# Layer 3 of a four-layer image network: gates ahead of another batch's taps, taps in PSUM, folding shared with GpSimd, a new order of two interleaved images

## The chip, the cores and the metric

The kernel runs on one core of one Trainium2 chip. The metric is the device time of one launch in microseconds (us), as the median of several runs. The core has a matrix engine (TensorE, PE in the profile, with its weight loads as PEld), a vector engine (VectorE, DVE), an activation engine (ScalarE, ACT), a general engine (GpSimd, POOL), a synchronisation engine (SyncE, SP) on whose queue this kernel issues its transfers, and 16 DMA engines. Each engine works through its own queue in order; semaphores make one wait for another. SBUF is the on-chip memory, PSUM the accumulation memory that TensorE writes.

## What is computed

Eight images of 192 channels and 64 x 64 pixels, in 32-bit floats, pass four layers. Layers 0 and 2 are two-dimensional state-space scans in four directions, with norms, 1 x 1 convolutions and gates around them. Layer 1 works pixel by pixel. Layer 3 is the one that the change touches:

```python
xc = _conv1x1(x, w1, b1)                       # 192 -> 64 channels
for nw in (4, 8, 12):
    s = H // nw; k = s + H % nw                # (s, k): (16, 16), (8, 8), (5, 9)
    hi = (jnp.arange(nw) * s)[:, None] + jnp.arange(k)[None, :]
    patches = xc[:, :, hi][..., hi]
    u3 = patches.transpose(0, 1, 3, 5, 2, 4).reshape(N, C * k * k, nw * nw)
    u4 = u3.reshape(-1, C, k, k)               # the same bytes, read as samples
    a = _se(_conv1x1(u4, w2, b2), wse1, wse2) + _dwconv3x3(u4, wpos, bpos)
    a3 = a.reshape(N, C * k * k, nw * nw)
    p = a3.reshape(N, C, k, k, nw, nw).transpose(0, 1, 4, 2, 5, 3)
    folded = jnp.zeros((N, C, H, W)).at[:, :, hidx, widx].add(p)
    out_list.append(folded / cnt)
out = _conv1x1(jnp.concatenate(out_list, axis=1) + x, w3, b3)
```

`_se` multiplies each sample by a sigmoid gate per channel, made from the sample's means by two small matrices; `_dwconv3x3` is a depthwise 3 x 3 convolution, nine taps per pixel.

## The kernel before

For each image there are a scan of layer 0, the end of layer 0 and layer 1, a scan of layer 2, and then `between(b, b + 1)`. The scans are ordered by hand and take most of the time. `between` is different: it interleaves two generators, `behind` for image b (the end of layer 2, all of layer 3, the output) and `ahead` for image b + 1 (the load, norm, dense 1 x 1 convolutions and depthwise convolution that open layer 0). The generators are stepped in turn, one step of each; the order in which they are stepped is the order in which the program is written, and a scheduler derives from it and from the buffers the fixed order of instructions on each queue. So there is one `ahead` without a partner at the start, seven mixed stages, and one `behind` without a partner at the end. A pool of PSUM is shared: a "wide" tile holds two rows of 512 floats, a "narrow" one holds one. In a mixed stage each generator has one wide and two narrow buffers, alone three and two.

`behind` first loads the four scan results (`ys`, L745, 6 MB), joins and norms them in four steps, and makes `xc` in four steps. It copies the windows with VectorE or ScalarE into `p2` and `p01` and stores them to `u3` in device memory (L793). The same bytes are read back as samples: this is what turns windows into samples. `samples(i, p, passes, t_u, t_p)` (L818) then does, for one pass, the following:

- loads the samples into `u4`, a view of the room named by `t_u` (L832), clears a padded tile in the room named by `t_p` on GpSimd (L836) and copies the samples into it with ScalarE (L838);
- for each group of samples multiplies by `w2` (L846), adds a bias in place (L850), and sums over pixels (L854); two small matmuls and a Sigmoid (L862) give the gate;
- for each group runs the nine taps: four on TensorE into a narrow PSUM tile (L870); GpSimd writes `acc` = u4 x gate (L876) and adds two terms that ScalarE makes (L884, L885); VectorE adds three taps to `acc` in SBUF (L887), and last combines PSUM, bias and `acc` into `u4` (L890);
- stores `u4` to `a3` in device memory (L897).

Window 2 goes in two passes of six groups, windows 0 and 1 in one pass of four each, twenty groups an image. A group is 128 partitions of 486 or 512 floats. There are five rooms, t0 to t3 and u, which the passes take in turn, so a load into a room waits for the store out of it. After the second pass window 2 is read back from `a3` (L795) and, after the third, added to a cleared image (memset L905) at its window positions by VectorE (L914, 18 instructions, nine rows of the window in two parts each), then scaled where windows overlap (L921, L924). After the fourth pass windows 0 and 1 are read back together into t0 and added to x (L932): window 0 by VectorE and GpSimd in alternation, window 1 by VectorE. Four steps of final matmuls (L939, L462, L465) and the output follow. `ahead` has its own dense convolution with stores to `a_scr`, its depthwise convolution (L1012 on TensorE, L1019 on VectorE in place in PSUM), stores to `vs` (L1026, L1058, L1060) and the transposed columns (`put_columns`, L1068 to L1078).

Of the kernel before, what the change touches and what calls it, by code (L numbers as in the profile page):

```python
# [7 lines left out]
F32 = mybir.dt.float32  # L8
AF = mybir.ActivationFunctionType
ALU = mybir.AluOpType  # L10
# [4 lines left out]
P = 128  # L15
CA, CB = 128, 64
S = 64
T = S * S
W = 1024
NCH = T // W  # L20
Q = 512
# [19 lines left out]
def tile_net(ctx: ExitStack, tc: tile.TileContext, a: dict, out: bass.AP):  # L41
    nc = tc.nc
# [23 lines left out]
    a3 = [dram.tile([64, k * k * nw * nw], F32, name=f"a3_{nw}") for nw, _, k in WINDOWS]  # L66
# [357 lines left out]
    def half(h):  # L424
        return slice(h * CB, (h + 1) * CB)
# [300 lines left out]
    PE_TAPS = 4  # L726


    def behind(b, pool, wk, psp, table):

        wide_, narrow_ = psp
        x = new_pair(pool, "x")

        def room(tag, n):
            return pool.tile([P, n], F32, name=tag, tag=tag)
# [45 lines left out]
        def view(flat, i, n=None):  # L781
            nw, s, k = WINDOWS[i]
            return flat.rearrange("p (a b i j) -> p a b i j", a=n or k, b=k, i=nw)

        def move_windows(i, t, dram, store):
            if i < 2:
                pairs = [(t[half(i)], dram[i])]
            else:
                pairs = [(t[half(0)], dram[2][:, 0 : 45 * 144])]
                pairs += [(t[half(1)][:, 0 : 36 * 144], dram[2][:, 45 * 144 :])]  # L790
            for s, d in pairs:
                if store:
                    nc.sync.dma_start(out=d, in_=s)  # L793
                else:
                    nc.sync.dma_start(out=s, in_=d)  # L795
# [19 lines left out]
            move_windows(i, p01, u3, True)  # L815


        def samples(i, p, passes, t_u, t_p):  # L818

            nw, s, k = WINDOWS[i]  # L820
            kk, nsmp = k * k, nw * nw
# [37 lines left out]
            ps = wide_("se2")[:, 0]  # L859
            nc.tensor.matmul(ps[:, :mh], se2, hid, start=True, stop=True)  # L860
            gate = wk.tile([P, mh], F32, tag="gate3", name="gate3")
            nc.scalar.activation(gate, ps[:, :mh], AF.Sigmoid)  # L862
            yield "pass"
            for g in range(0, mh, per):
                ms = slice(g, g + per)
                ps = narrow_("pw")
                tap = [divmod(t, 3) for t in range(9)]
                tap = [pad[:, g // per, dy : dy + k, dx : dx + k, :] for dy, dx in tap]
                for t in range(PE_TAPS):
                    nc.tensor.matmul(  # L870
                        ps[:, : per * kk], taps[:, t, :], tap[t],
                        start=(t == 0), stop=(t == PE_TAPS - 1),
                    )
                acc = wk.tile([P, Q], F32, tag="acc", name="acc")[:, : per * kk]
                turned = u4[:, ms, :].rearrange("p m j -> p j m")
                nc.gpsimd.tensor_tensor(  # L876
                    acc.rearrange("p (j m) -> p j m", m=per), turned,
                    gate[:, ms].unsqueeze(1).to_broadcast([P, kk, per]), ALU.mult,
                )
                rows = acc.rearrange("p (r x) -> p r x", r=k)  # L880
                tap = [t.rearrange("p r q m -> p r (q m)") for t in tap]
                for t in range(PE_TAPS, PE_TAPS + 2):
                    term = wk.tile([P, Q], F32, tag="term", name="term")[:, : per * kk]
                    nc.scalar.mul(term.rearrange("p (r x) -> p r x", r=k), tap[t], pos[:, t : t + 1])  # L884
                    nc.gpsimd.tensor_tensor(acc, acc, term, ALU.add)  # L885
                for t in range(PE_TAPS + 2, 9):
                    nc.vector.scalar_tensor_tensor(  # L887
                        rows, tap[t], pos[:, t : t + 1], rows, ALU.mult, ALU.add
                    )
                nc.vector.scalar_tensor_tensor(  # L890
                    turned, ps[:, : per * kk].rearrange("p (j m) -> p j m", m=per), bpos,
                    acc.rearrange("p (j m) -> p j m", m=per), ALU.add, ALU.add,
                )
                yield "conv"
            for h in range(2):
                m0 = h * (nsmp // 2) + p * mh
                nc.sync.dma_start(out=af[:, m0 : m0 + mh, :], in_=u4[half(h)])  # L897

        yield from samples(2, 0, 2, "u", "t2")
        yield from samples(2, 1, 2, "t0", "t1")  # L900
        p2 = room("t1", size["t1"])
        move_windows(2, p2, a3, False)
        yield from samples(0, 0, 1, "u", "t2")
        acc = room("t2", size["t2"])[:, 0:T]
        nc.gpsimd.memset(acc, 0.0)  # L905
        yield from samples(1, 0, 1, "t0", "t3")


        nw, s, k = WINDOWS[2]
        for ki in range(k):  # L910
            h = ki // 5
            for kj0, kj1 in ((0, s), (s, k)):
                to = image_rows(acc[half(h)], s, nw, ki, kj0, kj1)
                nc.vector.tensor_tensor(  # L914
                    to, to, view(p2[half(h)], 2, 5)[:, ki - 5 * h, kj0:kj1], ALU.add
                )
            yield "fold"

        both = acc[:, s * S : s * nw * S].rearrange("p (g r w) -> p g r w", r=s, w=S)
        both = both[:, :, 0 : k - s, :]  # L920
# [1 line left out]
        both = acc.rearrange("p (h w) -> p h w", w=S)[:, :, s : s * nw]  # L922
        both = both.rearrange("p h (g r) -> p h g r", r=s)[:, :, :, 0 : k - s]
        nc.vector.tensor_scalar_mul(both, both, 0.5)  # L924
        p01 = room("t0", size["t0"])
        for i in range(2):
            nw, s, k = WINDOWS[i]
            move_windows(i, p01, a3, False)
            for ki in range(k):
                to = image_rows(x[0][half(i)], s, nw, ki, 0, k)  # L930
                eng = nc.gpsimd if i == 0 and ki % 2 else nc.vector
                eng.tensor_tensor(to, to, view(p01[half(i)], i)[:, ki], ALU.add)  # L932
            yield "fold"
        two = w3[0][:, 320:384]
        for u in range(NU):
# [144 lines left out]
    def between(done, todo):  # L1080

        with (
            tc.tile_pool(name="bt_w", bufs=2) as wk,
            tc.tile_pool(name="bt_ps", bufs=1, space=PSUM) as psp,
            ExitStack() as stack,
        ):
            gens = []
            table = tc.keep_in_program_order(nc.scalar.preload_act_table_set(EXP_LN))
            alone = done is None or todo is None
            for name, fn, b in (("c", behind, done), ("a", ahead, todo)):  # L1090
                if b is None:
                    continue
                pool = stack.enter_context(tc.tile_pool(name="bt_" + name, bufs=1))

                def wide_(what, name=name):
                    return psp.tile(
                        [P, 2, Q], F32, tag="pa" + name, name=what + name, bufs=3 if alone else 1
                    )

                def narrow_(what, name=name):  # L1100
                    return psp.tile([P, Q], F32, tag="pb" + name, name=what + name, bufs=2)

                gens.append(fn(b, pool, wk, (wide_, narrow_), table))
            while gens:
                for g in list(gens):
                    if next(g, None) is None:
                        gens.remove(g)

    layer1_weights()
    between(None, 0)  # L1110
    for b in range(nimg):
# [131 lines left out]
```

## Time and profile before

| what | us |
|---|---|
| median of 3 runs (27051.87 to 27094.4) | 27072.46 |
| the profiled execution's own time | 27067.12 |
| its span | 27065.3 |
| first mixed stage, from the first load of ys to the next scan's first load | 471.4 (3071.97 to 3543.39) |
| the last image alone, from the first load of ys to the end | 367 (26698.29 to 27065.3) |

The times are in us from the start of the span. A group line of the profile names the line of the code, the engine, the operation, the tile written and the tiles read, the shape, how often it ran, its busy time and the mean of one in ns, and then the idle time of its engine just before it with what ended that. A line of the timeline has the start, the length, the engine and the group; the brackets hold the idle time before and what released it. A line of the table of waits has the engine and line that waited, the one waited for, the sum in us, how many times and the longest.

The engines' totals over the whole span:

```profile
PE 23913.7 (88%) x108424; PEld 10495.5 (39%) x108424; DVE 21238.1 (78%) x24245; ACT 14494.4 (54%) x23064; POOL 19174.4 (71%) x7516
```

They are averages over scans and stages between them: the scans fill TensorE, VectorE and GpSimd, the stages between them are emptier.

### The profile page before, as it was taken

Reading aid. Unit: us, or ns where it says so; the run is one execution under the profiler, and the core shown is the slowest. Engines: PE = TensorE matmul, PEld = TensorE weight load, DVE = VectorE, ACT = ScalarE, POOL = GpSimd, SP = SyncE. Lnnn points to the kernel's source line nnn. Section 1 sums busy time; section 2 is a strip of 40 time slices with the busy share of each in tenths; the row PEclk is TensorE's granted clock in tenths of the full one; section 3 lists DMA queues with packets and bytes.
Section 4 is the critical chain, followed back from the end, with each engine's and each line's share of the span. In section 5 each row is a group of like instructions: output and inputs, shape, how many; then the busy total and the mean of one; then the engine's idle time right before and its main releaser. Section 6 shows DMA issues by size and latency. Waiting matters only on the chain.

```text
span 27065.3 us, 306873 instructions
## 1 busy us (share of the span) xinstructions
PE 23913.7 (88%) x108424; PEld 10495.5 (39%) x108424; DVE 21238.1 (78%) x24245; ACT 14494.4 (54%) x23064; POOL 19174.4 (71%) x7516
## 2 busy tenths in 40 slices
PE   9979889798897988979889798897988979889797
PEld 3424334243342433424334243342433424344243
DVE  7959779597795978959789597895978959788596
ACT  5646556465564655646456464564645546455464
POOL 6929679295792957929579295792957939579395
PEclk8989989899898998989989899898998989989898
DMA  5636556265563655626556365563655636556364
GB/s 158 200 92 197 146 160 201 91 194 147 161 198 90 197 146 164 201 90 199 142 164 198 92 197 142 162 198 93 197 142 165 194 98 197 139 165 195 96 197 130
DMA packets 1239264, 4286.14 MB, mean 158 GB/s; under 512 B 427920, under 2 KB 454384, under 8 KB 839408
## 3 DMA queue, kind: packets, MB, share of 16 engines
q1 hardware_dynamic: 1237744, 4266.51, 53.5%
q8 instruction: 877, 14.37, 0.2%
q14 instruction: 643, 5.27, 0.1%
HBM read 3810.80 MB, written 450.72 MB: 157 GB/s over the span
## 4 chain that ended last, share of the span: by engine, by line
PE 29%; DVE 24%; issue 5%; POOL 5%; ACT 3%; DMA 2%; SPq 0%; DVEq 0%; POOLq 0%; ACTq 0%
DVE da L296 16%; PE py L326 10%; PE u L278 8%; POOL da L308 2%; PE pa L462 2%; DVE dg L193 1%; DVE u L293 1%; DVE tmp L291 1%; POOL acc L885 1%; PE pa L465 1%; PE misc L208 1%; ACT da L241 1%; POOL acc L876 1%; PE misc L226 1%; PE pac L462 1%
## 5 line engine op out<-in xcount | busy, mean ns | idle before, releaser
L308 POOL TENSOR_TENSOR da<-da,ct 128x2048 f32<-128x2048 f32 x3072 | 13920.5, 4531 | 856.9 <-DVE tmp L291 475.5
L296 DVE TENSOR_TENSOR_SCAN da<-da,u 128x1024 f32<-128x1024 f32 x6144 | 14046.0, 2287 | 447.4 <-ACT da L251 162.1
L326 PE MATMUL py<-da,ident 128*128 128x512 f32 x18432 | 9658.6, 642 | 59.9 <-POOL da L308 59.9
L278 PE MATMUL u<-dg,dtt 32*128 32x256 f32 x65536 | 7247.2, 410 | 663.5 <-DVE da L296 656.3
L241 ACT ACTIVATE da<-dt,neg_a 128x512 f32<-128x512 f32 x12288 | 7612.3, 708 | 16.3
L278 PEld LDWEIGHTS u<-dg,dtt 32*128 32x128 f32 x65536 | 4137.1, 164 | 5382.7 <-issue 3538.8
L326 PEld LDWEIGHTS py<-da,ident 128*128 128x128 f32 x18432 | 3258.5, 197 | 4117.5 <-issue 3958.1
L218 POOL TENSOR_TENSOR dtx<-dt,vt 128x512 f32<-128x512 f32 x768 | 979.0, 1276 | 4187.7 <-ACT dt L214 4017.4
L311 POOL TENSOR_TENSOR da<-da 128x512 f32<-128x512 f32 (+1 forms) x3072 | 3484.4, 1134 | 240.9
L228 ACT COPY dtt<-misc 128x512 f32<-128x512 f32 x768 | 450.1, 586 | 3001.5 <-PE misc L226 3001.5
L293 DVE TENSOR_TENSOR u<-u,tmp 128x16 f32<-128x16 f32 x6048 | 1106.2, 183 | 951.9 <-PE u L278 354.8
L231 ACT COPY dtt<-misc 32x512 f32<-32x512 f32 x3072 | 1772.1, 577 | 46.2
L193 DVE TENSOR_TENSOR dg<-msk,misc 128x1024 f32<-128x1024 f32 x1024 | 1223.3, 1197 | 251.5 <-PE misc L183 222.1
L155 ACT ACTIVATE xd<-misc,msk 128x512 f32<-128x512 f32 x256 | 176.0, 687 | 1806.9 <-PE misc L151 1806.9
L291 DVE TENSOR_TENSOR tmp<-da,da 128x16 f32<-128x16 f32 x5376 | 945.0, 176 | 144.7
L214 ACT ACTIVATE dt<-misc 128x512 f32<-128x512 f32 x768 | 430.7, 595 | 1055.7 <-PE misc L210 1010.7
L836 POOL MEMSET t<- 128x4356 f32 (+2 forms) x32 | 99.8, 3120 | 1186.2 <-DVE t L810 1029.7
L870 PE MATMUL pwc<-t,l3taps 128*128 128x486 f32 (+1 forms) x1280 | 723.1, 703 | 242.6 <-DVE u L890 144.5
L887 DVE SCALAR_TENSOR_TENSOR acc<-t,l3p,acc 128x486 f32<-128x486 f32 (+1 forms) x480 | 479.7, 1026 | 415.8 <-POOL acc L885 412.1
L141 PE MATMUL misc<-vt,wxt 128*128 128x512 f32 x512 | 318.0, 706 | 361.9 <-DMA vt<-vs 361.9
L208 PE MATMUL misc<-xd,wdt 64*128 64x512 f32 x1024 | 600.4, 699 | 13.4 <-ACT xd L155 13.4
L462 PE MATMUL pa<-sqa,mean_w 128*128 128x512 f32 x384 | 304.7, 939 | 344.5 <-ACT sqa L502 344.5
(285 smaller groups left out, 18922.6 us busy)
## 6 DMA issues: line engine op xcount, KB each, us to landing
ct<-cd SPq DMA_DIRECT2D x2048, 1024.0 KB
ct<-cd SPq DMA_DIRECT2D x2048, 512.0 KB
vt<-vs SPq DMA_DIRECT2D x768, 256.0 KB
yp<-yo SPq DMA_DIRECT2D x384, 256.0 KB
yo<-yp SPq DMA_DIRECT2D x384, 256.0 KB
ys<-yo SPq DMA_DIRECT2D x384, 256.0 KB
yt<-ys SPq DMA_DIRECT2D x96, 512.0 KB
t<-ys SPq DMA_DIRECT2D x96, 512.0 KB
```

The lines of the kernel that those rows point to most:

```text
L193: nc.vector.tensor_tensor(dg[m, o][:, at], msk[:, 0:32].unsqueeze(1).unsqueeze(1).to_broadcast(shape), bts[m, o][:, at, r * 8 : r * 8 + 8] ...
L218: nc.gpsimd.tensor_tensor(dtx[k], dts[k], vt[k // 3][:, units[k][3], :], ALU.mult)
L231: nc.scalar.copy(dtt[k][q * 32 : q * 32 + 32, 1], src if q < 3 else src[:, ::-1])
L241: nc.scalar.activation(das[k][:, :, n, :], dts[k].rearrange("p (s t) -> p s t", t=SB), AF.Exp, scale=neg_a[:, v, d, n : n + 1],)
L278: nc.tensor.matmul(u[ch, r * 8 : r * 8 + 8, e:SB:2], dtt[k][rows, r, w, e * P + ch.start : e * P + ch.stop], dg[k // 3, o][rows, i], start ...
L291: nc.vector.tensor_tensor(tmp, da0[:, k % 2, s, :], prev, ALU.mult)
L293: nc.vector.tensor_tensor(head, head, tmp, ALU.add)
L296: nc.vector.tensor_tensor_scan(h, h, u.rearrange("p n t -> p (n t)")[:, way], 0.0, ALU.mult, ALU.add)
L308: nc.gpsimd.tensor_tensor(h, h, cts.pop((k, g)), ALU.mult)
L311: nc.gpsimd.tensor_tensor(to, to, h[:, :, NS - n : NS], ALU.add)
L326: nc.tensor.matmul(py[k], ident, das[k][:, :, n, :], start=(n == 0), stop=(n == NP - 1))
L462: nc.tensor.matmul(pa[:, h], w[0][:, c], src[0][:, h], start=True, stop=False)
```

## The change

`samples` is cut in two. `gates` does everything up to the gate (the load, the padded tile, `w2`, the sums, the gate) and returns what the taps need; `convolve` is the generator that runs the taps of the groups and stores them. The order becomes: gates of pass 1, gates of pass 2, taps 1, gates 3, taps 2, gates 4, taps 3, and taps 4 after the fold of window 2. The Sigmoid is written as a Tanh with one more VectorE operation. The taps start in a wide PSUM tile; GpSimd adds one ScalarE term instead of two, and VectorE adds four taps, in place in PSUM, instead of three in SBUF. In the fold of window 2 GpSimd takes the rows 5 to 8, which lie in the other half of the partitions, in turn with VectorE's rows 0 to 4; in those of windows 0 and 1 it takes the odd rows. Window 0 is read back ahead of the fourth pass's taps and window 1 after them, into t1 instead of t0. In a mixed stage `behind` has two wide and one narrow PSUM buffer, `ahead` one and one. The generators are stepped in a new order: one step of `ahead`, thirteen of `behind`, and from then on two of `behind` for each of `ahead`.

```diff
-        def samples(i, p, passes, t_u, t_p):
+        def gates(i, p, passes, t_u, t_p):
...
-            nc.scalar.activation(gate, ps[:, :mh], AF.Sigmoid)
-            yield "pass"
+            nc.scalar.activation(gate, ps[:, :mh], AF.Tanh, scale=0.5)
+            nc.vector.tensor_scalar(gate, gate, 1.0, 0.5, ALU.add, ALU.mult)
+            return k, kk, mh, per, u4, pad, gate, [(af, h * (nsmp // 2) + p * mh) for h in range(2)]
+
+        def convolve(k, kk, mh, per, u4, pad, gate, to):
             for g in range(0, mh, per):
                 ms = slice(g, g + per)
-                ps = narrow_("pw")
+                ps = wide_("pw")[:, 0]
...
-                rows = acc.rearrange("p (r x) -> p r x", r=k)
                 tap = [t.rearrange("p r q m -> p r (q m)") for t in tap]
-                for t in range(PE_TAPS, PE_TAPS + 2):
-                    term = wk.tile([P, Q], F32, tag="term", name="term")[:, : per * kk]
-                    nc.scalar.mul(term.rearrange("p (r x) -> p r x", r=k), tap[t], pos[:, t : t + 1])
-                    nc.gpsimd.tensor_tensor(acc, acc, term, ALU.add)
-                for t in range(PE_TAPS + 2, 9):
+                term = wk.tile([P, Q], F32, tag="term", name="term")[:, : per * kk]
+                nc.scalar.mul(
+                    term.rearrange("p (r x) -> p r x", r=k), tap[PE_TAPS], pos[:, PE_TAPS : PE_TAPS + 1]
+                )
+                nc.gpsimd.tensor_tensor(acc, acc, term, ALU.add)
+                rows = ps[:, : per * kk].rearrange("p (r x) -> p r x", r=k)
+                for t in range(PE_TAPS + 1, 9):
                     nc.vector.scalar_tensor_tensor(
                         rows, tap[t], pos[:, t : t + 1], rows, ALU.mult, ALU.add
                     )
...
-        yield from samples(2, 0, 2, "u", "t2")
-        yield from samples(2, 1, 2, "t0", "t1")
+        first = gates(2, 0, 2, "u", "t2")
+        yield "gates"
+        second = gates(2, 1, 2, "t0", "t1")
+        yield "gates"
+        yield from convolve(*first)
+        third = gates(0, 0, 1, "u", "t2")
+        yield "gates"
+        yield from convolve(*second)
         p2 = room("t1", size["t1"])
         move_windows(2, p2, a3, False)
-        yield from samples(0, 0, 1, "u", "t2")
+        fourth = gates(1, 0, 1, "t0", "t3")
+        yield "gates"
+        yield from convolve(*third)
         acc = room("t2", size["t2"])[:, 0:T]
         nc.gpsimd.memset(acc, 0.0)
-        yield from samples(1, 0, 1, "t0", "t3")
...
-        for ki in range(k):
+        for ki in (0, 5, 1, 6, 2, 7, 3, 8, 4):
             h = ki // 5
             for kj0, kj1 in ((0, s), (s, k)):
                 to = image_rows(acc[half(h)], s, nw, ki, kj0, kj1)
-                nc.vector.tensor_tensor(
+                (nc.gpsimd if h else nc.vector).tensor_tensor(
                     to, to, view(p2[half(h)], 2, 5)[:, ki - 5 * h, kj0:kj1], ALU.add
                 )
...
-        p01 = room("t0", size["t0"])
+        p01 = room("t1", size["t1"])[:, 0:T]
+        move_windows(0, p01, a3, False)
+        yield from convolve(*fourth)
+        move_windows(1, p01, a3, False)
         for i in range(2):
             nw, s, k = WINDOWS[i]
-            move_windows(i, p01, a3, False)
             for ki in range(k):
                 to = image_rows(x[0][half(i)], s, nw, ki, 0, k)
-                eng = nc.gpsimd if i == 0 and ki % 2 else nc.vector
-                eng.tensor_tensor(to, to, view(p01[half(i)], i)[:, ki], ALU.add)
+                (nc.gpsimd if ki % 2 else nc.vector).tensor_tensor(
+                    to, to, view(p01[half(i)], i)[:, ki], ALU.add
+                )
             yield "fold"
...
-                    return psp.tile(
-                        [P, 2, Q], F32, tag="pa" + name, name=what + name, bufs=3 if alone else 1
-                    )
+                n_wide, n_narrow = (3, 2) if alone else ({"a": 1, "c": 2}[name], 1)
...
+            order = "a" + "c" * 13
             while gens:
-                for g in list(gens):
-                    if next(g, None) is None:
-                        gens.remove(g)
+                for name in order:
+                    if name in gens and next(gens[name], None) is None:
+                        del gens[name]
+                order = "cca"
```

In the changed file the GpSimd product is L880, the ScalarE term and its addition up to L889, VectorE's taps L892, the combination L895, the fold of window 2 L926, the scaling L934 and L937, the last folds L946, and `ahead`'s depthwise taps L1035.

## The prediction

> **What bounds the kernel now.** I read the page first, for the totals, then the table of windows over the first of the seven stages that mix layer 3 of one image with layer 0 of the next (3071.97, the first load of ys, to 3543.39, the next scan's first load: 471 us; the other six last 470 each, the last image alone 367), then its waits, and last the timeline of the last image, where layer 3 stands without a neighbour. The scans, the remaining 23,400 us, are not touched.
>
> ```profile
> span 27065.3 us, 306873 instructions
> ...
> L887 DVE SCALAR_TENSOR_TENSOR acc<-t,l3p,acc 128x486 f32<-128x486 f32 (+1 forms) x480 | 479.7, 1026 | 415.8 <-POOL acc L885 412.1
> ```
> ```profile
> 3293.00:3349.00 56.00, 41.68 (x93) 15.36 (x92) 33.65 (x40) 26.52 (x36) 28.03 (x19) 0.88 0.31 81
> ...
> 3457.00:3498.00 41.00, 15.04 (x24) 5.25 (x24) 17.13 (x17) 4.50 (x7) 17.28 (x12) 0.62 0.27 61
> ...
> 3069.00:3546.00 477.00, 328.91 (x777) 109.52 (x776) 260.00 (x307) 169.05 (x203) 114.52 (x75) 0.82 0.41 92
> ```
> ```profile
> POOL acc L876 <- ACT gate L862: 116.5, 4, 56.2
> ...
> DVE acc L887 <- POOL acc L885: 51.4, 15, 8.9
> ...
> PE pac L462 <- DVE xa L932: 30.0, 1, 30.0
> ```
> ```profile
> 26838.65 5.26 POOL L885 TENSOR_TENSOR acc<-acc,term 128x486 f32<-128x486 f32 x4
> ...
> 27019.59 8.48 POOL L932 TENSOR_TENSOR xa<-xa,t 64x256 f32<-64x256 f32 x8 [19.88 <-DMA t<-a]
> ```
> ```profile
> 26841.19 5.15 DVE L887 SCALAR_TENSOR_TENSOR acc<-t,l3p,acc 128x486 f32<-128x486 f32 x5 [7.73 <-POOL acc L885]
> ...
> 26946.82 22.46 DVE L914 TENSOR_TENSOR t<-t,t 64x720 f32<-64x720 f32 x18 [1.71 <-POOL t L905]
> ...
> 27019.55 16.23 DVE L932 TENSOR_TENSOR xa<-xa,t 64x256 f32<-64x256 f32 x16 [13.88 <-DMA t<-a]
> ```
> ```profile
> 26873.48 3.52 SPq L897 DMA_DIRECT2D a<-u  x2
> 26890.34 1.27 SPq L832 DMA_DIRECT2D u<-u  x2
> ```
> In the window rows the columns are PE, PEld, DVE, ACT, POOL busy, clock, DMA share, GB/s. The fullest engine of the stage, PE, is busy 329 of 477 us: chains bound it. The chain is gate (56 us of idle POOL before the first), taps handed from POOL to DVE, fold, store and reload, fold, final matmuls. The last pair shows a store whose tile is loaded anew 16.9 us later.
>
> **What the Trainium skill says.** "SBUF — State Buffer", Who interferes with whom: a VectorE instruction with two SBUF inputs contends with a GpSimd instruction that reads SBUF, one with at most one SBUF input doesn't. The trace agrees: L887, both inputs in SBUF, takes 696 to 1987 ns (median 740, mean 1026), L1019, the same operation into PSUM, 734 to 757 in all 320. "GPSIMD Engine Reference", Elementwise — side-by-side cycle accounting, has GpSimd near half of VectorE's speed for two inputs; here 1208 ns at least for L885 against 696 for L887. "ScalarE: Activation LUTs", What ACT_TABLE_LOAD costs: about 1283 ns for the load, the same for every set; this trace has exactly 1283, 15 times at L862.
>
> **The change part by part.**
>
> *Taps.* Twenty groups an image. Before, POOL made 1.53 + 2 x 1.27 = 4.1 us of each and DVE three taps, mostly after POOL; conv of six groups took 41 us in the mixed stage and 32 alone (26841.2 to 26873.4), 5.4 each. Now DVE has four taps at 0.73 to 0.756 (the L1019 row) and L890's 1.05: 4.0 us; POOL 1.53 + 1.27 = 2.8; PE's four taps 4 x 0.70 = 2.8 to 3.6. DVE becomes the bound, 24 to 25 us for six groups: -8 alone, -16 where the neighbour's work sat in between. Two PSUM buffers let PE run one group ahead. ACT makes one term of 0.72 fewer a group, off the path.
>
> *Gates ahead.* The first two are made before the first conv, so the second's 10 us (26873.4 to 26884.2) go under loads. The third and fourth are not free: they load into u and t0, which the first and second conv have to have stored. Their reductions stand in DVE's order, and their matmuls in PE's, ahead of the next conv. Price, from the trace of the last image: 16.9 from store to load issue, 8 to land, 5 for reductions and gate, is 30 us from conv 1 to conv 2; from conv 2 to conv 3 also the p2 reload (2.9 MB at about 210 GB/s, 14 us) lies ahead in the queue: 44. Before, these waits lay under another conv. The table loads save 15 x 1.3 = 19 us at most, 8 on the path; the Tanh's extra DVE operation costs 0.1 each.
>
> *Order of the two images.* The next image's first step is issued before ys, 3 MB ahead of its 6 MB: the first norm is about 19 us later. Then thirteen steps of layer 3 come with nothing of the neighbour's dense work between them, and with two wide buffers instead of one. In the built order of instructions xc ends about 3180 (3193 before), the u3 writes are issued together from 3193 (before, one half at 3200 and the rest at 3225 and 3230, behind the a_scr stores on SP's queue), u is loaded at 3220, the first gate matmul falls at 3226 instead of 3273, and conv 1 runs 3261 to 3286 (before 3293 to 3334). The neighbour's dense and depthwise work, with one PSUM buffer of each kind (a group's matmuls 3.65 us, then DVE's 3.9, in turn), fills the two load gaps: 3286 to 3326 and 3354 to 3398. So conv 2 is at 3326 to 3354, conv 3 at 3398 to 3415: 9 us before the old 3424.
>
> *Folding.* New waits: L934's scaling on DVE waits for POOL's half, with the rest of conv 4's taps queued behind it, and the reload of window 0, now into t1, waits for both halves (SP has only conv 4's store behind it). For window 2, DVE keeps 10 of 18 instructions, 10 x 1.33 = 13.3 us; POOL takes 8. Its price is not in the trace. From below: in the shared fold of L932 a pair took 1.06 while DVE alone needs 0.58, so 0.48 for 256 elements, and 1.2 for a mean of 648; from above, L885's 1.21 for 486 scaled, 1.6. If the two exclude each other, as L932 says, the fold is 13.3 + (9.8 to 12.9) = 23 to 26 us, against 22.5; I take 24.5, a gain of nothing in itself. What helps is that conv 4's taps, with one SBUF input, run beside it: before, fold, scaling, gate and conv 4 were a row of 59 us (3424 to 3483); now the memset (3.5, now bare), the fold and conv 4 (16) overlap in 37 to 45. I take 41: -18. The store and reload before the last fold, 14.8 us, stays. Fold 0 (8 x 0.9 = 7 us) is done under it; fold 1 shared is 4 x 1.14 + 4 x 1.0, 9 as before: -7 for the tail. One narrow buffer instead of two in the final four steps: +0 to 4, taken +2.
>
> *Sum of a mixed stage:* -9 at conv 3, -18, -7, +2 = -32; I write -29, since 3 us of waits in hand-offs between queues are surely missed. Bounds: -36 to -18. Seven: -203 (-252 to -126).
>
> *The last image* has no neighbour to fill the gaps. Conv 1 begins about 4 us later (26845) and ends 3 earlier, conv 2 is 26905 to 26928 instead of 26884 to 26916, conv 3 ends about 26989 instead of 26945; the overlap and fold 0 win back 25: +10 (-20 to +25).
>
> Sum: -193, so 27067.1 (the profiled execution: span 27065.3 plus 1.8) becomes 26,874. The median of the runs shown, 27072.46, lies 5 above this base; 26,875 for either.
>
> **Rivals.**
>
> *The stages overlap better.* The window table leaves PE 148 us idle, and the load gaps are shorter if stores land faster than 16.9. With gaps of 30 and 30 and fold beside conv 4 in 30, conv 3 ends 14 earlier and the tail 11: -55 a stage, -20 alone, 26,662. Against it: the depthwise work of the neighbour is serial in its one buffer.
>
> *No gain.* The gates wait for store and load, the lock makes the shared fold cost 26 and delays POOL's operations for conv 4, and conv 3 ends where it ended: stages at -3 to +3, 27,065. For it: the edits that look like gains, gates ahead and sharing, each hit a wait that the trace prices.
>
> *Slower.* One mechanism: the reloads of u and t0. SP's queue is in order; the L832 that waits for its store holds the neighbour's vs stores behind it (L1026 and L1058 in this queue), these hold its staging tiles, and so DVE's and PE's depthwise work, which stands ahead of conv 2 and 3 in their orders. It decides once conv 3 ends later than 3443 (3415 plus the 28 won otherwise). At +10 us in each gap and +19 from the late norm not won back, +20 a stage and +15 alone: 27,222. Against it: before, this queue already stood for 13 us in front of a reload (3392.6 to 3405.7), and DVE ran conv 3 meanwhile.
>
> **How the numbers follow.** Forecast 0.60; better overlap 0.18; no gain 0.12; slower 0.10. A measurement of this kernel tells 0.2%, 54 us, from no change. The forecast's and the first rival's cases are all faster by more; of the third a third is, so faster 0.82, same 0.08, slower 0.10. The forecast's own range is 26,800 to 26,970. To hold 8 in 10 it goes down to the better overlap and up to where no gain begins: 26,660 to 27,040.
>
> **What would show it.** Right: L892 at 0.72 to 0.76 with no wait for POOL's acc; L885's successor L889 once a group; the first scan load after the first mixed stage at 3507 to 3525; gaps of 30 to 45 us without taps of layer 3 between conv 1, 2 and 3; L926 on DVE and POOL together 23 to 26 us; no shorter stage for the last image. Wrong: POOL's and DVE's L926 each at their lone speed, conv 2 straight after conv 1, or the mixed stages longer than 470.

## The result, and the profile after

The changed kernel takes 27045.51 us (median of 20 runs, 27012.64 to 27073.03), the kernel before 27080.04 (20 runs, 27042.47 to 27104.11). The ratio is 0.9987, with a 95% interval of 0.9981 to 0.9994: a gain of 0.13%, 35 us, where 193 were forecast and 27,040 was the upper end of the range.

The scans vary by some 50 us between executions (23,376 to 23,425 us for everything outside the stages in the profiles below), so the stages are what to compare. A stage is counted here from the end of the scan's last VectorE addition to the next scan's first load, or, for the last image, to the end of the span. Within one kernel the seven mixed stages agree to some 6 us.

| profile | mean of the seven mixed stages | last image alone | all eight |
|---|---|---|---|
| before | 472.3 | 369.1 | 3675.1 |
| after | 461.9 | 408.2 | 3641.6 |

So each mixed stage became 10.4 us shorter (73 in all) and the last one 39 longer; the difference, 34, is as much as the medians differ. The page of after, for the totals, and two rows of its costliest groups:

```profile
span 27048.6 us, 306720 instructions
...
L880 POOL TENSOR_TENSOR acc<-u,gate 128x486 f32<-128x486 f32 (+1 forms) x80 | 108.5, 1360 | 965.8 <-DVE u L895 690.6
L874 PE MATMUL pwc<-t,l3taps 128*128 128x486 f32 (+1 forms) x1280 | 595.1, 614 | 198.4 <-DVE t L895 188.9
```

and the row of VectorE's taps among all groups by line:

```profile
L892 DVE SCALAR_TENSOR_TENSOR pwc<-t,l3p,pwc 128x486 f32<-128x486 f32 (+1 forms) x640 | 466.9, 735 | 84.0 <-PE pwc L874 69.9
```

The taps do what was meant. Before, VectorE idled 416 us ahead of its taps and one took 1026 ns; now 640 instead of 480 of them take less time together, 735 ns each, and the wait for GpSimd's `acc` is gone. But GpSimd now has 966 us of idle time ahead of its product L880 in the passes that use u. The same row of the kernel before has 634:

```profile
L876 POOL TENSOR_TENSOR acc<-u,gate 128x486 f32<-128x486 f32 (+1 forms) x80 | 116.5, 1465 | 633.5 <-ACT gate L862 536.7 <-DVE u L890 96.8
```

This idle time costs nothing in itself; it tells where the passes wait.

The table of windows of after shows where, in the first mixed stage (columns: the window and its length, busy time of PE, PEld, DVE, ACT, POOL, clock, DMA share, GB/s). The first and second row are the gaps between the taps of passes 1 and 2 and of 2 and 3, the third goes from the end of the third pass's taps to the end of the fourth's, the last is the stage:

```profile
3293.80:3337.90 44.10, 35.04 (x78) 13.20 (x78) 23.04 (x34) 10.80 (x16) 4.16 (x3) 0.85 0.49 70
...
3364.30:3420.60 56.30, 38.02 (x89) 13.59 (x90) 25.75 (x36) 17.64 (x23) 2.38 (x2) 0.73 0.90 180
...
3437.80:3487.60 49.80, 17.46 (x41) 5.91 (x40) 49.40 (x41) 2.46 (x4) 44.47 (x23) 0.73 0.23 50
...
3076.70:3540.60 463.90, 316.62 (x776) 105.34 (x776) 260.54 (x319) 155.62 (x182) 117.63 (x67) 0.83 0.42 94
```

In the second gap the DMA engines are busy 0.90 of the time, VectorE less than half, and TensorE is granted 0.73 of its clock. In the third VectorE and GpSimd are both full, 49.4 and 44.5 of 49.8 us, and it is only 9 us shorter than the 59 that it replaced.

The last image has no neighbour to fill the gaps, so its timeline shows them bare. VectorE (start, length, engine, group, and in brackets the idle time before and what ended it), from the last tap of pass 1 to the first of pass 2, and from the last of pass 2 to the first of pass 3:

```profile
26826.77 1.04 DVE L895 SCALAR_TENSOR_TENSOR u<-pwc,l3p,acc 128x486 f32<-128x486 f32 x1
26855.34 0.69 DVE L854 TENSOR_REDUCE pool<-u 128x2 f32<-128x512 f32 x1 [27.52 <-ACT u L850]
...
26863.31 3.02 DVE L892 SCALAR_TENSOR_TENSOR pwc<-t,l3p,pwc 128x486 f32<-128x486 f32 x4 [3.10 <-PE pwc L874]
...
26884.35 1.04 DVE L895 SCALAR_TENSOR_TENSOR t<-pwc,l3p,acc 128x486 f32<-128x486 f32 x1
26928.13 2.59 DVE L854 TENSOR_REDUCE pool<-t 128x8 f32<-128x512 f32 x4 [42.74 <-ACT t L850]
...
26935.37 3.13 DVE L892 SCALAR_TENSOR_TENSOR pwc<-t,l3p,pwc 128x512 f32<-128x512 f32 x4 [3.24 <-PE pwc L874]
```

and SyncE's queue in the same time:

```profile
26827.88 3.52 SPq L901 DMA_DIRECT2D a<-u  x2
26844.27 1.27 SPq L832 DMA_DIRECT2D u<-u  x2
26885.45 3.68 SPq L901 DMA_DIRECT2D a<-t  x2
26901.79 1.13 SPq L795 DMA_DIRECT2D t<-a  x2
26902.96 15.55 SPq L832 DMA_DIRECT2D t<-u  x2
```

The taps of pass 1 end, `u` is stored, 16.4 us later its room is loaded with the samples of pass 3, and only after that pass's gate do the taps of pass 2 begin, though all that they need has been there for long. From taps to taps it is 35.5 us (26827.8 to 26863.3), and 50 the second time (26885.4 to 26935.4), where the 2.9 MB of window 2 go through the queue ahead of the samples.

### The profile page after: what moved, and what is told of

It reads as the page before. It is cut to its first block, busy times and chain, and to the rows that moved or that the text cites. A ratio compares the mean times of both kernels' runs of the same rounds, so it can differ in the third digit from the quotient of the medians.

```text
span 27048.6 us, 306720 instructions
## 1 busy us (share of the span) xinstructions
PE 23842.9 (88%) x108424; PEld 10470.0 (39%) x108424; DVE 21240.1 (79%) x24341; ACT 14390.5 (53%) x22904; POOL 19197.4 (71%) x7452
## 4 chain that ended last, share of the span: by engine, by line
PE 29%; DVE 26%; issue 5%; ACT 3%; POOL 3%; DMA 2%; SPq 0%; DVEq 0%; POOLq 0%; ACTq 0%
DVE da L296 17%; PE py L326 10%; PE u L278 8%; PE pa L462 2%; DVE dg L193 2%; DVE u L293 2%; POOL da L308 1%; DVE tmp L291 1%; PE pa L465 1%; PE misc L208 1%; ACT da L241 1%; PE misc L226 1%; PE misc L183 1%; DVE pwc L892 1%; DMA a<-t 1%
## 5 line engine op out<-in xcount | busy, mean ns | idle before, releaser
L880 POOL TENSOR_TENSOR acc<-u,gate 128x486 f32<-128x486 f32 (+1 forms) x80 | 108.5, 1360 | 965.8 <-DVE u L895 690.6
L874 PE MATMUL pwc<-t,l3taps 128*128 128x486 f32 (+1 forms) x1280 | 595.1, 614 | 198.4 <-DVE t L895 188.9
```

## The experiments

Stage lengths are read as above. A kernel that was run once has its one time beside one of the kernel before that was taken with it. How far a stage length can be trusted is seen where two kernels have the same instructions in the same order in a stage: the last image differs by 3.6 us between e4 and e12 and by 3.4 between e8 and e10, the mean of the mixed stages by 2.5 between after and e5 and by 0.4 between e4 and e10. Smaller differences than these show nothing.

| kernel | mixed | alone | time, kernel before beside it |
|---|---|---|---|
| e1 taps alone | 434.7 | 339.1 | 26802, 27107 |
| e2 order alone | 462.7 | 367.5 | 27008, 27107 |
| e3 change, folds as before | 460.2 | 404.6 | 27039, 27107 |
| e4 change, gates late | 409.4 | 342.3 | 26611, 27107 |
| e5 change, own rooms in the last image | 459.4 | 343.2 | 26947, 27088 |
| e6 e4, second gates ahead | 418.3 | 376.0 | 26700, 27088 |
| e7 e4, third and fourth gates ahead | 447.7 | 391.0 | 26925, 27088 |
| e8 e4, folds as before | 410.8 | 336.5 | 26619, 27088 |
| e9 taps and order | 425.9 | 339.2 | 26698, 27078 |
| e10 e4, last image's folds as before | 409.8 | 339.9 | 26615.8, 27077.6 |
| e11 e4, fourth taps ahead of the fold | 409.2 | 345.6 | 26615, 27078 |
| e12 e4, PSUM as before | 509.4 | 338.7 | 27297, 27078 |

**e1, the kernel before with the new taps alone**, in a narrow PSUM tile, of which there are two.

```diff
-                rows = acc.rearrange("p (r x) -> p r x", r=k)
-                for t in range(PE_TAPS, PE_TAPS + 2):
+                for t in range(PE_TAPS, PE_TAPS + 1):
...
-                for t in range(PE_TAPS + 2, 9):
+                rows = ps[:, : per * kk].rearrange("p (r x) -> p r x", r=k)
+                for t in range(PE_TAPS + 1, 9):
```

> The kernel before with the new taps alone: one ScalarE term and one GpSimd addition a group, four VectorE taps in place in PSUM. Stage lengths are from the scan's last VectorE addition to the next scan's first load: 472 us mixed and 369 alone before, 462 and 408 with the whole change. Theory A (the gates ahead of other taps cost the last image its time, the taps are a gain): alone 345 to 350, since each conv of six groups falls from 32 to 25 and each of four from 20 to 17; mixed 450 to 460; the span about 130 us shorter. Theory B (taps do not set the stages' length, other waits do): both within 3 us of before.

Mixed 434.7 and alone 339.1: -37.6 and -30.0, more than theory A had. One part of the change alone brings 293 us in the stages, nearly nine times the whole change.

**e2, the kernel before with the new order of steps alone.**

```diff
+            order = "a" + "c" * 13
             while gens:
-                for g in list(gens):
+                for name in order:
...
+                order = "cca"
```

> The kernel before with the new order of steps alone (one of the next image, thirteen of layer 3, then two to one), PSUM buffers as before. It cannot touch the last image: 369 us. Theory A: conv 1 of layer 3 starts earlier by 10 to 30 us in the mixed stages, but the later waits give part of it back: mixed 455 to 468. Theory B (the 3 MB loaded ahead of ys and the neighbour's work pushed to the end cost more than they give): mixed above 475.

Mixed 462.7, -9.6, and the last image, which has the same instructions, within 2 us: theory A. The 3 MB loaded ahead of ys cost less than the order brings.

**e3, the whole change with the folds of before.**

```diff
-                (nc.gpsimd if h else nc.vector).tensor_tensor(
+                nc.vector.tensor_tensor(
...
-                (nc.gpsimd if ki % 2 else nc.vector).tensor_tensor(
+                (nc.gpsimd if i == 0 and ki % 2 else nc.vector).tensor_tensor(
```

> The whole change, but the folds of window 2 and window 1 on VectorE alone as before. Theory A: sharing is a small loss, VectorE and GpSimd alternate: window 2's fold 26.4 us shared, 22.5 alone; mixed and alone both 1 to 5 us shorter than with the whole change (462 and 408). Theory C (the shared folds are where the gain went): 10 us or more shorter. Theory D (sharing helps as meant): 3 us or more longer.

Mixed -1.7 and alone -3.6 against the whole change: inside theory A's numbers, but no more than the same instructions differ between two runs. So sharing gains nothing, and a loss isn't shown. The two engines' durations show why. The line of the fold, after (min, median, max in ns):

```profile
L926 DVE TENSOR_TENSOR t<-t,t x80: 1273/2898/3324, 3441.1 to 26980.7; 64x720 f32<-64x720 f32 x40, 64x576 f32<-64x576 f32 x40
L926 POOL TENSOR_TENSOR t<-t,t x64: 2540/2816/3226, 3441.8 to 26976.0; 64x720 f32<-64x720 f32 x32, 64x576 f32<-64x576 f32 x32
```

and in e3, where VectorE has all 18 instructions:

```profile
L926 DVE TENSOR_TENSOR t<-t,t x144: 1161/1315/2336, 3423.9 to 26970.0; 64x720 f32<-64x720 f32 x72, 64x576 f32<-64x576 f32 x72
```

Ten of the 18 instructions, each at twice the duration.

**e4, the whole change with each pass's gates right ahead of its own taps.** The fourth pass's gates stand ahead of the fold; its taps still follow it.

```diff
         first = gates(2, 0, 2, "u", "t2")
...
-        second = gates(2, 1, 2, "t0", "t1")
...
         yield from convolve(*first)
-        third = gates(0, 0, 1, "u", "t2")
+        second = gates(2, 1, 2, "t0", "t1")
...
         yield from convolve(*second)
...
-        fourth = gates(1, 0, 1, "t0", "t3")
+        third = gates(0, 0, 1, "u", "t2")
...
         yield from convolve(*third)
...
+        fourth = gates(1, 0, 1, "t0", "t3")
```

> The whole change, but each pass's gates written right ahead of its own taps (the fourth after the third taps, ahead of the fold), as before. Theory A: this takes the waits of 36 and 50 us between the convs of the last image down to some 10 each and lets conv 1 start 16 us earlier: alone 345 to 360 instead of 408; mixed 440 to 458 instead of 462. Theories B and C: alone and mixed within 5 us of the whole change.

Mixed 409.4 and alone 342.3: the way of theory A, and below its range both times, in the mixed stage by 31 us. The gates ahead cost 52.5 us in each mixed stage and 66 in the last, 433 in all. In e4 the store of `u` and the reload of its room lie under the taps of pass 2. Its SyncE queue in the last image stores u at 26434.15 and reloads the room at 26450.24, while VectorE runs the second pass's taps from 26441.4 to 26463.5.

**e5, the whole change, where in the last image the third and fourth pass have rooms of their own.** In the mixed stages, where the rooms of `ahead` stand beside these, it wasn't tried.

```diff
...
-        third = gates(0, 0, 1, "u", "t2")
+        third = gates(0, 0, 1, "v0" if last else "u", "t2")
...
-        fourth = gates(1, 0, 1, "t0", "t3")
+        fourth = gates(1, 0, 1, "v1" if last else "t0", "t3")
```

> The whole change, but in the last image (where SBUF has the space) the third and fourth pass load their samples into rooms of their own, so that these loads wait for no store. The order of all instructions is else the same. Theory A1 (the price of gates ahead is the wait for the store of the tile that is loaded anew): the waits of 36 and 50 us between the convs of the last image fall below 12 each, part of it comes back as a wait for the reload of window 2 ahead of its fold; alone 350 to 370 instead of 408. Theory A2 (it is the length of the gate work itself and its place ahead of the taps in the queues, whatever the load waits for): alone above 395. Mixed stages as with the whole change, 462.

Alone 343.2 instead of 408.2, so the same gain as from moving the gates back, and 7 us more than A1 had: theory A1, and for the last image the end of A2. The gates keep their place, and what their load waits for is taken away. The two gaps between the taps, 35.5 and 50.0 us in after, are 15.7 and 9.2 here, which is 60.6 of the 65 us. (Behind them the built order differs: two groups and a part of the third of pass 4 stand ahead of the fold.) VectorE from taps 1 to taps 2 (L896 is L895 of after, L893 L892, L855 L854):

```profile
26786.17 1.04 DVE L896 SCALAR_TENSOR_TENSOR u<-pwc,l3p,acc 128x486 f32<-128x486 f32 x1
26793.14 1.87 DVE L855 TENSOR_REDUCE pool<-v 128x2 f32<-128x512 f32 x3 [5.92 <-ACT v L851]
...
26802.88 3.02 DVE L893 SCALAR_TENSOR_TENSOR pwc<-t,l3p,pwc 128x486 f32<-128x486 f32 x4 [4.68 <-PE pwc L875]
```

The idle time ahead of the reductions falls from 27.5 to 5.9 us; the 15.7 that are left from taps to taps are these waits, the gate work itself and the next group's taps on TensorE.

This run also shows the two engines one after the other. VectorE's fold and GpSimd's instructions beside it:

```profile
26862.33 11.09 DVE L927 TENSOR_TENSOR t<-t,t 64x720 f32<-64x720 f32 x9
```
```profile
26862.50 11.99 POOL L890 TENSOR_TENSOR acc<-acc,term 128x512 f32<-128x512 f32 x1
26874.56 15.64 POOL L927 TENSOR_TENSOR t<-t,t 64x720 f32<-64x720 f32 x8
```

An addition that takes GpSimd 1.27 us elsewhere took 11.99, as long as VectorE's fold lasted. After it, GpSimd's eight instructions of the fold took 15.64, so one every 1.96 us.

**e6 and e7, gates late with one half of them ahead again.**

```diff
         first = gates(2, 0, 2, "u", "t2")
         yield "gates"
-        yield from convolve(*first)
         second = gates(2, 1, 2, "t0", "t1")
         yield "gates"
+        yield from convolve(*first)
         yield from convolve(*second)
```

> The kernel with gates late (mixed 409, alone 342), with the second pass's gates alone written ahead of the first taps again; that load waits for no store. Theory A1: a loss of 10 to 18 us alone, since conv 1 stands behind the second load; mixed 409 to 418. Theory A2: the same loss for each pass, a third of the total: alone 358 to 368, mixed 422 to 430.

```diff
         second = gates(2, 1, 2, "t0", "t1")
         yield "gates"
+        third = gates(0, 0, 1, "u", "t2")
+        yield "gates"
         yield from convolve(*second)
...
-        third = gates(0, 0, 1, "u", "t2")
+        fourth = gates(1, 0, 1, "t0", "t3")
         yield "gates"
         yield from convolve(*third)
...
-        fourth = gates(1, 0, 1, "t0", "t3")
-        yield "gates"
```

> The kernel with gates late, with the third pass's gates written ahead of the second taps and the fourth's ahead of the third taps again; the second's stay late. Theory A1: most of the loss is here: alone 385 to 400, mixed 445 to 465. Theory A2: two thirds of the loss: alone 380 to 390, mixed 440 to 448. Theory E (the second gates are the harm in the mixed stage, since all later work is shifted by them): mixed below 425.

e7: mixed +38.3 and alone +48.7 against e4, both inside A1's numbers; A2's hold the mixed one too, and miss the other by 1. e6: mixed 418.3 (+8.9), at the edge of A1's numbers and below A2's; but alone 376.0 (+33.7), above both, where A1 had 10 to 18. Its timeline tells why: the load that waits for no store costs the start (first tap 26485.9, 24.8 after the first gate, in e4 4.2), but the two sets of taps then run back to back, nothing covers the store of `u`, and the reload of its room falls in with window 2's 2.9 MB:

```profile
26532.28 5.98 SPq L832 DMA_DIRECT2D u<-u  x1
26545.48 1.13 SPq L795 DMA_DIRECT2D t<-a  x2
26546.65 0.60 SPq L832 DMA_DIRECT2D u<-u  x1
```
```profile
26569.28 0.69 DVE L854 TENSOR_REDUCE pool<-u 128x2 f32<-128x512 f32 x1 [40.89 <-ACT u L850]
```

So the wait for the store moved by one pass. A1 names the cause; its estimate for e6 left out that gate work between the taps also covers a store.

**e8, gates late and the folds of before** (the two edits of e3 and e4).

> Gates late, and the folds of window 2 and of window 1 on VectorE alone. Theory A: sharing is a small loss by itself, so alone 336 to 342 against 342. In the mixed stages, VectorE now has work of the neighbour that could run while GpSimd folds: mixed 400 to 412 against 409. Theory D (sharing pays once the gates are out of the way): mixed 413 or more.

Alone -5.8, mixed +1.4: inside theory A's numbers. The -5.8 is in part chance, since e10 has the same last image and 339.9. From the end of pass 3's taps to the end of pass 4's the last image takes 64.9 us in e4 and 64.2 in e12, with the fold shared, and 61.2 and 61.7 in e8 and e10, without. So with late gates sharing loses some 3 us there; in the whole change it makes no difference (42.7 in after, 42.5 in e3). The mixed stage is level.

**e9, the kernel before with the taps of e1 and the order of e2.**

> The kernel before with the new taps and the new order of steps together, nothing else. The taps alone took 37.6 us off a mixed stage, the order alone 9.6. Theory A (they add, since they act on different parts of the stage): mixed 422 to 428, alone 339. Theory F (the order pays more once the taps are short): mixed 409 to 416, and then the rest of the change, PSUM buffers and the fold, is worth nothing.

Mixed 425.9, theory A: they add (472.3 - 37.6 - 9.6 is 425.1).

**e10, gates late, folds on VectorE in the last image but for the odd rows of window 0.**

> Gates late, folds shared in the mixed stages, on VectorE in the last image except the odd rows of window 0: the best of each stage that the runs so far show. Mixed 409, alone 337, the time 1.6 to 1.8% below the kernel before, 26,590 to 26,640 us.

26615.8 us (four runs, 26604.48 to 26634.76), ratio to the kernel before 0.9827, interval 0.9811 to 0.9844. Alone it is 339.9 instead of the expected 337, with e8's last image. It beats both kernels; against e4, one run at 26611, nothing is won by it.

**e11, gates late, the fourth pass's taps ahead of the fold.**

```diff
         fourth = gates(1, 0, 1, "t0", "t3")
         yield "gates"
+        yield from convolve(*fourth)
...
         move_windows(0, p01, a3, False)
-        yield from convolve(*fourth)
```

> Gates late, with the fourth pass's taps written ahead of the fold of window 2 instead of after it. Theory A (the fold beside the fourth taps is a gain, as predicted, about 10 us): mixed 417 to 425, alone 348 to 355. Theory G (where the fold stands is worth nothing, VectorE does the one after the other in any case): both within 4 us of 409 and 342.

409.2 and 345.6 against 409.4 and 342.3: theory G's numbers, but not a test of it. The taps were written ahead of the fold and built behind it all the same. VectorE in the last image of e11 (L927 is the fold):

```profile
26495.38 14.18 DVE L927 TENSOR_TENSOR t<-t,t 64x720 f32<-64x720 f32 x10 [2.44 <-POOL t L918]
...
26542.26 3.11 DVE L892 SCALAR_TENSOR_TENSOR pwc<-t,l3p,pwc 128x512 f32<-128x512 f32 x4
```

In e4 it is the same, fold at 26493.84 and first tap at 26539.98, and so it is in the first mixed stage of both. What the place of the fold among the taps is worth stays open.

**e12, gates late, PSUM in the mixed stage as before.**

```diff
-                n_wide, n_narrow = (3, 2) if alone else ({"a": 1, "c": 2}[name], 1)
+                n_wide, n_narrow = (3, 2) if alone else (1, 2)
```

> Gates late, with PSUM in the mixed stages as before: one wide and two narrow buffers for each image, so that a group's taps on TensorE wait until VectorE has finished the group before. The last image is the same, 342. Theory A (VectorE is the bound of the taps only because a second buffer lets TensorE run ahead): mixed 425 or more, about 3 us for each of the 20 groups not covered by the neighbour. Theory G (the neighbour's work fills these waits): mixed 405 to 415.

Mixed 509.4, +100: theory A, and 5 us a group instead of 3. The waits of the first mixed stage from the gates on name it; the same row has 12.4 us in e4:

```profile
DVE pwc L892 <- PE pwc L874: 70.3, 13, 7.1
```

`gates` and `convolve` take all their PSUM from the wide buffers, so with one of them TensorE can't start a group, or a gate's matmul, before VectorE is done with the group before. Taps in the two narrow tiles, as in e1, don't need the second wide buffer.

**The sum.** From before to after, step by step; the third step holds four things together:

| step | mixed | alone |
|---|---|---|
| before | 472.3 | 369.1 |
| taps in PSUM, one term less (e1) | -37.6 | -30.0 |
| order of steps (e9 less e1) | -8.8 | +0.1 |
| PSUM buffers, fold, Tanh, reload in two parts (e4 less e9) | -16.5 | +3.1 |
| gates ahead (after less e4) | +52.5 | +65.9 |
| after | 461.9 | 408.2 |

What makes the -16.5 in the third step isn't settled. Sharing gives nothing (e8), and the buffers can't be judged alone, since wide taps with one buffer (e12) are a new bound. Most of it is there before the fold: in the mean of the mixed stages the taps of pass 1 end 26 us earlier in e4 than in e9, those of pass 3 20 earlier. The Tanh is a candidate that no run tests alone: ScalarE loads its function tables 695 times in e9 and 632 times in e4, 63 times fewer in seven stages, at 1.283 us each. The alone values of the second and third step are no more than the same instructions differ.

## Why the prediction was wrong

*Taps: right, and larger than priced.* Forecast were 24 to 25 us for six groups; the first mixed stage of after has 24.8 for conv 1 (3269.0 to 3293.8), the last image 22.1 for conv 2. The term "-8 alone" for six groups was the right size: for 20 groups it gives 27, and e1 has 30 in the last image. In the mixed stage the taps alone were worth 37.6.

*Gates ahead: the step that failed.* "Price, from the trace of the last image: 16.9 from store to load issue, 8 to land, 5 for reductions and gate, is 30 us from conv 1 to conv 2; from conv 2 to conv 3 ... 44." They measured 35.5 and 50. The chain and its places were right, and so was the price up to the landing: the samples were there 24.3 us after the taps of pass 1 in the last image (24.9 in the price), 38.2 after those of pass 2 (38.9), and 38.9 in the first mixed stage. The term that failed is "5 for reductions and gate": from the samples to the next tap it took 11.2 and 11.8 us in the last image, and 17.4 in the second gap of the first mixed stage:

```profile
3403.14 3.95 ACT L838 COPY t<-t 128x512 f32<-128x512 f32 x4 [6.62 <-DMA t<-u]
3407.84 1.28 DVE L854 TENSOR_REDUCE pool<-t 128x8 f32<-128x512 f32 x2 [16.87 <-DMA vs<-ha]
3414.59 0.18 DVE L864 TENSOR_SCALAR gate<-gate 128x32 f32<-128x32 f32 x1 [1.50 <-ACT gate L863]
3420.61 3.13 DVE L892 SCALAR_TENSOR_TENSOR pwc<-t,l3p,pwc 128x512 f32<-128x512 f32 x4 [5.84 <-PE pwc L874]
```

The 5 begins at the first reduction. Ahead of that stand the first matmul with `w2` and its bias (4.7 us here, 3.2 and 4.6 in the last image), and behind the gate TensorE has to make the first group's four taps (5.8 here, 3.1 and 3.2 in the last image). What is longer in the mixed stage is TensorE's work, and there it was granted a lower clock. From the samples to the next tap, in this gap and in the second of the last image (the number before the last two is the clock):

```profile
3403.10:3420.60 17.50, 14.71 (x21) 5.71 (x22) 2.83 (x5) 7.56 (x11) 0.00 (x0) 0.53 0.63 210
26923.50:26935.40 11.90, 10.01 (x21) 4.20 (x22) 2.77 (x6) 6.77 (x10) 0.00 (x0) 0.85 0.00 0
```

In the seven mixed stages this clock was 0.53 to 0.83 and the gap 56.3 to 52.9 us, where 44 was forecast; why it was lower isn't shown. In the first gap, 44.1 against 40, the load was issued 22.9 us after the store (3293.8 to 3316.6), behind a store of the neighbour's (L1042) that stood in SyncE's queue until 3316.2, waiting for its data. And the neighbour's work could not fill the second gap: on VectorE it ended at 3391, 16.9 us before the first reduction.

*"Conv 1 begins about 4 us later" in the last image.* Measured from the scan's end, its first tap came at 165.3 instead of 145.0 us: 20 later. The second pass's reductions stand ahead of it in VectorE's order, and wait 12.2 us for samples that land later than the first pass's. The prediction had put them "under loads". In the mixed stage the same place was forecast well: 3286 for the end of conv 1, against 3286.8 when the later start of this stage (7 us) is taken off.

*Folding: the lock was named rightly, its price was too low, and work of VectorE was put at nothing.* "From below ... 1.2 for a mean of 648; from above ... 1.6" for GpSimd: e5 has 1.96. "23 to 26 us" for the fold: 24.4 for nine of VectorE's ten, 26.5 to the end of the last. And "conv 4's taps, with one SBUF input, run beside it" did not happen: nine of VectorE's ten instructions stand in a row in its queue, each waits its turn with GpSimd, and most of the taps wait behind them. From the end of conv 3 to that of conv 4 it was 49.8, where 41 was taken and 37 to 45 given. The 41 is about the fold (24.5) and conv 4 (16) one after the other; in the same queue stand the two scalings (4.1 us) and VectorE's half of window 0's additions (6.5), which "is done under it" counted as free. The tail after it came out as forecast, 53.0 us for 60 before.

*Table loads: nothing saved.* At the gate they fell from 15 to 1, but the whole trace has 632 of them, as before: the norms (L505 and L506) have 37 instead of 16.

*Order, window copies and PSUM: right.* e2's -9.6 is what the order alone leaves at the stage's end, of the 32 us that it brings at the end of conv 1. Without the second wide buffer (e12) the stage is 100 us longer.

*A slip in the sum of the last image.* Conv 3 was to end at 26989 instead of 26945, 44 later, and 25 were to be won back: that is +19, not the +10 that went into the sum. Measured from the start of the stage, conv 3 ended 63 later, and 24 were won back.

*Range and rivals.* The time lies in the rival "No gain", but by another split: its stages were to be at -3 to +3, and they are at -10.4 and +39. Its cause was half of the true one: gates ahead hit the store of the tile that is loaded anew. Its other half, "conv 3 ends where it ended", is near too: conv 3 ended 7 us later than before when the later start of the stage is taken off (3430.8 against 3424.1), and 16 later than forecast. A mixed stage came out 18.6 us longer than forecast and the last image 29, together 159 of the 193. In the first mixed stage the two gaps are 16 us of this and the fold with conv 4 9, less some 6 that other terms and the allowance for hand-offs give back; in the last image the start of conv 1 is 16, the slip in the sum 9 and the second gap 6, less 2 elsewhere (its times for conv 1 and 2 already had 35 for the first gap).

The prediction also never compared the parts. It set gains against losses in one walk along the queues, so that "Gates ahead" stood as two gaps with a price, and not as a loss of 52 us a mixed stage, which is what it is against the same kernel without it (e4).

## What to carry to other kernels

Work made ahead is only ahead if what it reads is there: when its load goes into a buffer that the work before still has to store, the "early" step puts the whole turnaround of store and load, and then its own work, in front of work that was ready, because the queues are in order. In the last image that was 35.5 and 50 us. Give it a buffer of its own, or leave it behind the work that covers its store. And measure a change of many parts by its parts: one of them here was alone worth nearly nine times the whole. And before a run that moves work is read, look whether the built order moved with the written one: in e11 it didn't.

## What the runs showed of the hardware

Two engines that both read two SBUF tensors took turns instruction by instruction: VectorE's 64-partition additions went from 1315 to 2898 ns and GpSimd's from 2042 (e5, after VectorE's fold) to 2816 ns (medians). The Trainium skill, "SBUF — State Buffer", Who interferes with whom, says that these contend; the same page, Summary: rules for kernel authors, that the second to issue is blocked until the first finishes. The alternation in after agrees. But a turn was not always had after one instruction: in e5 one GpSimd addition was held for 11.99 us while nine of VectorE's ran in 11.09, one every 1.23, as if alone. A store followed by a load into the same tile cost 16.1 (e4) to 16.9 us (before) from the issue of the one to that of the other, for 1.5 MB, in the last image, where nothing else stood between them in the queue. And the clock granted to TensorE for the same gate and taps was 0.53 in one gap of after and 0.85 in another, with 17.4 and 11.8 us from the samples to the next tap.
